# Four-layer convolution and scan network: order of work in layer 1's stream, one stream for layer 3, and the order of two ScalarE instructions

## The chip, the cores and the metric

The kernel runs on one core of a Trainium2 chip. The metric is the device time of one execution in microseconds (us), and the time that counts is the median of several executions. Five engines take part, each with its own instruction queue in program order: TensorE (PE in the profile, its weight loads PEld), VectorE (DVE), ScalarE (ACT), GpSimd (POOL) and SyncE (SP), which here does nothing but issue DMAs. An instruction waits on semaphores until what it needs is there, and everything behind it on its engine waits too. All data are float32.

## The reference, cut to what matters

The input is x of 8 x 64 x 64 x 64 (batch, channels, height, width). Four layers follow each other. Layer 0 (layer norm, FFTs, mixing) and the convolutional parts of layer 2 are not touched by the change. What the change touches are the selective scans. Layer 1 has this core, for 4 scan directions k of 8 images, 128 channels, 4096 tokens and 16 states:

```
xm = silu(dwconv3x3(ln(x) @ in_w)) ; z = second half of ln(x) @ in_w
dts, B, C = split(x_proj[k] @ xs[k]) ; delta = softplus(dt_w[k] @ dts + dt_b[k])
for each token: h = exp(delta*A)*h + delta*B*u ;  y = sum over states of h*C
y = ln(sum over the 4 directions of y + D*u) * silu(z) ; x1 = x + y @ out_w
x1 + conv1x1(gelu(h1) * h2)         # h1, h2 = dwconv3x3(conv1x1(ln(x1)))
```

Layer 3 has two stages, first along one axis of the image (s = 0), then along the other (s = 1). Stage 1 reads what stage 0 wrote. Each stage runs two Mamba blocks over sequences of 64 tokens, k = 0 forward and k = 1 backward, with 256 inner channels and 16 states:

```
xn = rms_norm(x) ; xc, z = split(xn @ in_w[k]) ; xc = silu(causal_conv(xc))
dts, B, C = split(xc @ xproj[k]) ; dt = softplus(dts @ dtw[k] + dtb[k])
h = h*exp(dt*A) + dt*xc*B ; y = (sum over states of h*C + D*xc) * silu(z)
out = concat(x + y0 @ out_w0, x + y1 @ out_w1) @ lin + linb + x
```

## The kernel before, in words

The whole network is one Python program that writes out every engine's instructions by hand. The scans of layers 1, 2 and 3 share the function `stream` (from L428 on). Its unit is a **tile**: one of the 16 states (n = 0 to 15) of one **step**, 128 channels x 1024 tokens (in layer 3 two halves of 512 tokens, one per half of the 256 channels). For tile i the stream issues:

- SP loads B's and C's row of this state, broadcast to 128 partitions. In layer 1 these are two loads of 512 KB, `b` by `fetch` (5 tiles ahead, 4 buffers) and `c` by `fetch_c` (3 tiles ahead, 5 buffers); in layers 2 and 3 one load brings both, and `fetch_c` does nothing.
- GpSimd multiplies `hb = du * b` (L484), 2 tiles ahead in layer 1 and 3 in the others.
- ScalarE computes `dA = exp(dt * A[n])` into PSUM (L491), 2 tiles ahead, in two buffers.
- VectorE scans `h = dA * h + hb` (L500).
- `h * C` (L514, `multiply_c`) is done by VectorE, except in the tiles called shared (n = 1, 4, 7, 10, 13 as a rule; 2, 6, 10, 14 in one step out of four in layer 3), where GpSimd does it one tile later.
- TensorE adds the product into the step's sum `acc` by a matmul with the identity (L306, `gather`), two tiles later. After the 16th tile VectorE takes the sum out (`drain`).

The next step's inputs are made while the present one is scanned: `prepare` is a Python generator that is advanced one piece per tile from n = `start` on (2 in layer 1, 1 in layer 3). It issues projection matmuls, ScalarE's copy `dbl`, the store of B and C to DRAM, softplus (`dt`), GpSimd's `du = dt * u` and, in layer 3, the matmuls of z and Silu(z).

Everything else in a layer is cut into pieces as well and queued as tasks in `behind`: in layer 1 `begin` (norm, convolution and z of an image ahead), `finish` (output norm, gate and projection of a finished image) and `feed` (its feed-forward part); in layer 3 `begin` (squares, mean, reciprocal root and `xn` of the next chunk; a chunk is 4 groups x 2 directions = 8 steps = 128 tiles). `advance` moves the first task on by one piece, once per tile. A piece ends in a `yield`, whose value says whether the task holds the shared PSUM buffer `mm` (True), needs one next (None), or neither (False). A task that said True is kept in `self.held`; no other work takes that buffer before it is done. `room` says whether a piece may take or hold PSUM in this tile: not while the preparation holds it. At n = `start` the preparation needs the buffer, so the loop `while self.held or self.urgent` runs the held task on, piece after piece in the same tile, until it lets go. These forced pieces stand ahead of the tile's scan in VectorE's queue. `late` is True for layer 1 alone, and there `early` is 8.

The pieces of layer 1 that the prediction names: L364 and L1065 are matmuls ahead of VectorE's L1011, L1104 and L1067; L1062 is a GpSimd product that L1067 also needs. In `feed`, a group is three matmul pieces (L917 twice, then L925), an empty piece, and its consumer: Gelu on ScalarE (L1130), a VectorE product (L1133), or Gelu (L1141), an empty piece and a VectorE product (L1144).

Layer 3 is the function `l3_stage`, called once per stage (L1815, L1816). Each call opens its own pools, loads and builds its weights, zeroes its buffers `raw` and `inv`, runs `begin(0)` to its end, and then runs a stream of 256 steps. At the end of `prepare` (L2013 to L2017) ScalarE first overwrites the last token of each sequence in `dt` with 1e30 (so that exp gives 0 there and the scan starts afresh at the next sequence), and then computes Silu(z). The overwriting must wait until `du` has been computed from the true `dt`.

The functions that the diff touches, with the profile's line numbers:

Of the kernel before, what the change touches and what calls it, by code (L numbers as in the profile page):

```python
# [268 lines left out]
class Net:  # L269
# [163 lines left out]
    def stream(self, pools, ahead, steps, behind, rest=None):  # L433
# [105 lines left out]
        for i in range(total + 2):  # L539
            at, n = divmod(i, NS)  # L540
            need(i + ahead[0], "bc")
            need(i + ahead[1], "du")
            fetch(i + ahead[0])
            fetch_c(i + ahead[2])
            multiply_b(i + ahead[1])
            if 0 < i <= total and shared(i - 1):
                multiply_c(i - 1)


            first = i > NS and n == 2  # L550
            late = i > 1 and not first and steps[0].late and shared(i - 2)
            if i > 1 and not late and not first:
                gather(i - 2)
            if at + 1 < len(steps) and n == steps[at].start:
                steps[at + 1].ready()
                while self.held or self.urgent:
                    self.advance(behind)
                work = Task(steps[at + 1].prepare())
            if work is not None and not (self.held and work.said is None) and (calm(i) or not work.calm):
                work.step()  # L560
                if work.over:
                    work = None
            room = work is None or work.said is not True and (n < steps[0].early or hasattr(steps[at + 1], "du"))
            self.advance(behind, room, calm(i))
            if late:
                gather(i - 2)
            if i < total:
                scan(i)
            if first:
                gather(i - 2)  # L570
            if i < total:
                if not shared(i):
                    multiply_c(i)
            decay(i + 2)
# [1239 lines left out]
    def layer3(self, src, dst):  # L1814
        self.l3_stage(0, src, self.hbm["x4"])  # L1815
        self.l3_stage(1, self.hbm["x4"], dst)  # L1816

    def l3_stage(self, s, src, dst):
# [5 lines left out]
        W, H = 512, 512 // HW  # L1824
        with ExitStack() as ctx:
            pool = lambda n, b, **k: ctx.enter_context(tc.tile_pool(name=f"l3{s}{n}", bufs=b, **k))
# [5 lines left out]
            def stage(name):  # L1832

                w = self.d["l3_" + name][:, 2 * s : 2 * s + 2]
                t = cp.tile(list(w.shape), F32, name="w_" + name)
                nc.sync.dma_start(t, w)
                return t

            linb = self.load(cp, "l3_linb")
            nw, w_in, cb, xp, dtw, dtb, A, D, w_out = (  # L1840
                stage(n) for n in ("nw", "in", "cb", "xp", "dtw", "dtb", "A", "D", "out")
            )
            lin = stage_lin = cp.tile([C, 2, C], F32, name="w_lin")
            nc.sync.dma_start(stage_lin, self.d["l3_lin"][:, s])
            self.minus_exp(A)
            nc.vector.tensor_scalar(A, A, -1e-27, None, ALU.min)
            skip = [self.diag(cp, f"skip{k}", D[:, k, :], 2) for k in range(2)]


            taps = [cp.tile([128, 2, 256], F32, name=f"taps{k}") for k in range(2)]  # L1850
            w_z = cp.tile([C, 2, 256], F32, name="w_z")
            w_end = cp.tile([128, 2, 2, C], F32, name="w_end")
            for k in range(2):
                for m in range(2):
                    for r in range(2):
                        row = self.d["l3_taps"][2 * s + k, m, r : r + 1, :]
                        nc.sync.dma_start(taps[k][r * C : r * C + C, m, :], row.to_broadcast([C, 256]))
                for m in range(2):
                    nc.vector.scalar_tensor_tensor(
                        taps[k][:, m, :], w_in[:, k, :256], nw[:, k : k + 1], taps[k][:, m, :], ALU.mult, ALU.mult  # L1860
                    )
                nc.vector.tensor_scalar(w_z[:, k, :], w_in[:C, k, 256:], nw[:C, k : k + 1], None, ALU.mult)

                for j in range(2):
                    ps = pp.tile([128, T], F32, name="mm")
                    nc.tensor.matmul(ps[:, :C], w_out[:, k, j * 128 : j * 128 + 128], lin[:, k, :], start=True, stop=True)
                    nc.scalar.copy(w_end[:, k, j, :], ps[:, :C])
            w_res = cp.tile([C, C], F32, name="w_res")
            nc.vector.tensor_tensor(w_res, lin[:, 0, :], lin[:, 1, :], ALU.add)
            nc.vector.tensor_tensor(w_res, w_res, self.ident[:C, :C], ALU.add)  # L1870
# [3 lines left out]
            nc.vector.memset(endless, 1e30)  # L1874

# [8 lines left out]
            def begin(c):  # L1884
# [4 lines left out]
                hold = chunks[c] = {"x": x}  # L1889
                from_ = src[q, rows, part * 4 * W : (part + 1) * 4 * W].rearrange("p (s t) -> p s t", t=HW)  # L1890
# [5 lines left out]
                for j in range(2):  # L1896
                    yield CALM_FREE
                    sq = p1.tile([C, T], F32, name="sq")
                    o = sq.rearrange("p (s t) -> p s t", t=HW)
                    nc.scalar.activation(o, x[:C, j * 2 * H : (j + 1) * 2 * H, ends[0]], AF.Square)  # L1900
                    yield
                    ps = pp.tile([128, T], F32, name="mm")
                    self.mm(ps[:1, :], mean, sq)
                    yield CALM
                    ms = p1.tile([1, T], F32, name="ms")
                    nc.scalar.copy(ms, ps[:1, :])
                    yield False
                    nc.sync.dma_start(rs[j * 64 : j * 64 + 64], ms.rearrange("o (p e) -> o p e", e=16))
# [30 lines left out]
            class Step:  # L1939
# [6 lines left out]
                def __init__(self, c, g, k):  # L1946
                    self.c, self.g, self.k, self.rev = c, g, k, k == 1
                    self.shared = (2, 6, 10, 14) if k and g % 2 else (1, 4, 7, 10, 13)
                    self.lanes = [(slice(j * W, j * W + W), A[:, k, j, :]) for j in range(2)]

                def ready(self):

                    while begun.get(self.c) in behind:
                        net.advance(behind)

                def prepare(self):
                    k, hold = self.k, chunks[self.c]
# [6 lines left out]
                    for j in range(2):  # L1964
                        for m, f in enumerate((4, 6) if k else (3, 1)):
                            nc.tensor.matmul(  # L1966
                                tokens(px[:, j * W : j * W + W]),
                                taps[k][:, m, j * 128 : j * 128 + 128],
# [7 lines left out]
                    for j in range(2):  # L1976
                        at = slice(j * W, j * W + W)
                        nc.scalar.activation(u[:, at], px[:, at], AF.Silu, bias=cb[:, k, j : j + 1])  # L1978
                    pd = pp.tile([128, T], F32, name="mm")[:36, :W]
                    for j in range(2):  # L1980
                        nc.tensor.matmul(pd, xp[:, k, j, :], u[:, j * W : j * W + W], start=j == 0, stop=j == 1)  # L1981
# [7 lines left out]
                    for j in range(2):  # L1989
                        nc.tensor.matmul(  # L1990
                            pt[:, j * W : j * W + W], dtw[:, k, j * 128 : j * 128 + 128], dbl[0:4], start=True, stop=True
# [4 lines left out]
                    for j in range(2):  # L1996
                        at = slice(j * W, j * W + W)
                        net.softplus_act(dt[:, at], pt[:, at], dtb[:, k, j : j + 1])
# [4 lines left out]
                    for j in range(2):  # L2003
                        nc.tensor.matmul(
                            tokens(pz[:, j * W : j * W + W]),
                            w_z[:, k, j * 128 : j * 128 + 128],
                            xn[:C, :, 3 : 3 + HW],
# [4 lines left out]
                    yield CALM  # L2012

                    at = HW - 1 if k else 0
                    nc.scalar.copy(dt.rearrange("p (s t) -> p s t", t=HW)[:, :, at], endless)
                    z = self.z = p2.tile([128, T], F32, name=f"z{k}")
                    nc.scalar.activation(z, pz, AF.Silu)  # L2017
# [5 lines left out]
                def skip(self, acc):  # L2023
                    for j in range(2):
                        at = slice(j * W, j * W + W)
                        nc.tensor.matmul(acc[:, at], skip[self.k][:, j, :], self.u[:, at], start=True, stop=False)
                    return True

                def drain(self, acc):
                    nc.vector.tensor_tensor(self.z, acc, self.z, ALU.mult)  # L2030
                    chunks[self.c][f"y{self.k}"] = self.z

                def done(self):
                    c, g = self.c, self.g
                    if self.k == 1:
                        net.urgent.append(Task(finish(c, g, [chunks[c]["y0"], chunks[c]["y1"]])))
                    if self.k == 0 and g == 0 and c + 1 < 2 * NB:
                        begun[c + 1] = Task(begin(c + 1))
                        behind.append(begun[c + 1])

            def finish(c, g, ys):
# [3 lines left out]
                x = chunks[c]["x"][:C, g * H : g * H + H, ends[0]]  # L2045
                nc.tensor.matmul(ps.rearrange("p (s t) -> p s t", t=HW), w_res, x, start=True, stop=False)  # L2046
                for k in range(2):
                    for j in range(2):
                        nc.tensor.matmul(  # L2049
                            ps, w_end[:, k, j, :], ys[k][:, j * W : j * W + W], start=False, stop=k == 1 and j == 1  # L2050
# [5 lines left out]
                if first:  # L2056
                    images[b] = p1.tile([C, L if s == 0 else 4 * W], F32, name="out")
# [10 lines left out]
            net = self  # L2068
            with tc.manual_schedule():
                Task(begin(0)).run()  # L2070
                steps = [Step(c, g, k) for c in range(2 * NB) for g in range(4) for k in range(2)]
# [27 lines left out]
```

## Time and profile before

| | us |
|---|---|
| median of 3 runs | 24834.52 (24824.01 to 24847.65) |
| the profiled execution's own time | 24819.55 |
| its span, first to last instruction | 24817.8 |
| layer 0 and the start of layer 1 | 0 to 1230 |
| layer 1, scan tiles (2,048) | 1230 to 8477 |
| rest of layer 1 and layer 2's first part | 8477 to 8957 |
| layer 2, scan tiles (512) | 8957 to 10617 |
| layer 2's last parts, start of layer 3 | 10617 to 11521 |
| layer 3, stage 0, scan tiles (2,048) | 11521 to 18125 |
| between the stages | 18125 to 18202 |
| layer 3, stage 1, scan tiles (2,048), and the end | 18202 to 24818 |

Busy time of the engines in three of these stretches, with the granted TensorE clock (1 is full speed) and the rate of the DMAs:

| stretch | length | PE | DVE | ACT | POOL | clock | GB/s |
|---|---|---|---|---|---|---|---|
| layer 1, tiles | 7247 | 6152 | 6656 | 3910 | 6728 | 0.93 | 317 |
| layer 3, stage 0 | 6604 | 5711 | 6409 | 4477 | 6511 | 0.95 | 170 |
| between the stages | 77 | 35 | 6 | 19 | 18 | 0.61 | 94 |

How such lines are read. A line of a view in order of time has the start and the length in us, the engine, the line of the kernel, the operation, what it writes and what it reads, a count (several of a kind are merged), and in brackets how long the engine stood idle before it and what released it. A line of the waits has who waited, for whom, the total in us, how often, and the longest. The page has, per engine, busy us, share of the span and number of instructions, and a digit string with the busy share in tenths in 40 slices of 620 us.

### The profile page before, as it was taken

How to read it: one execution, taken by the hardware profiler on the slowest of the kernel's cores; microseconds unless marked ns; L12 is line 12 of the kernel's file. 1: busy time of each engine (PE TensorE's matmuls, PEld its weight loads, DVE VectorE, ACT ScalarE, POOL GpSimd, SP SyncE). 2: the span in 40 equal slices, each digit the busy share in tenths (PEclk: the TensorE clock that was granted, in tenths of full speed). 3: DMA queues.
4: the chain of work that ended last, by engine and by line, in shares of the span. 5: the costliest groups of instructions: out<-in, count | busy, mean ns of one | idle time of the engine just before them, and what ended most of it. 6: DMA issues, size and time to landing. Idle time of an engine off the chain costs nothing. (4 is left out here: it accounts for less than half of the span.)

```text
span 24817.8 us, 193238 instructions
## 1 busy us (share of the span) xinstructions
PE 21209.1 (85%) x53146; PEld 8277.5 (33%) x53146; DVE 22437.6 (90%) x12958; ACT 14770.8 (60%) x18827; POOL 22097.5 (89%) x10583
## 2 busy tenths in 40 slices
PE   8877888888888888888888888888878888888888
PEld 6522333333333323322333333333323333333333
DVE  5399999999999679978999999999989999999999
ACT  4355555555555456624666666666666666666666
POOL 0199999999999669977999999999989999999999
PEclk9889999999999999999999999999989999999999
DMA  2399899899889669933455555555545554555454
GB/s 65 88 324 326 310 320 319 310 319 318 313 315 317 225 224 344 339 87 98 168 172 169 173 169 171 169 173 170 168 156 173 168 173 167 173 168 174 168 173 158
DMA packets 1835374, 5282.70 MB, mean 213 GB/s; under 512 B 533792, under 2 KB 540004, under 8 KB 1831984
## 3 DMA queue, kind: packets, MB, share of 16 engines
q1 hardware_dynamic: 1809712, 5207.00, 61.9%
q10 hardware_dynamic: 24576, 63.33, 0.7%
q8 instruction: 423, 6.93, 0.1%
q14 instruction: 663, 5.43, 0.1%
HBM read 5112.85 MB, written 156.11 MB: 212 GB/s over the span
## 5 line engine op out<-in xcount | busy, mean ns | idle before, releaser
L484 POOL TENSOR_TENSOR hb<-du,bc 128x1024 f32<-128x1024 f32 x4608 | 10745.6, 2359 | 201.3 <-DVE h L500 142.5
L306 PE MATMUL acc<-hc,ident 128*128 128x512 f32 x18560 | 8793.2, 615 | 109.8 <-DVE img L1266 61.4
L491 ACT ACTIVATE dA<-dt,w_A 128x512 f32<-128x512 f32 x8192 | 5655.4, 691 | 3950.7 <-DVE hc L514 2884.6
L500 DVE TENSOR_TENSOR_SCAN dA<-dA,hb 128x1024 f32<-128x1024 f32 x3320 | 7578.5, 2283 | 227.9 <-ACT dA L491 151.0
L306 PE MATMUL acc<-h,ident 128*128 128x512 f32 x8064 | 4623.7, 702 | 2390.1 <-POOL h L514 2361.7
L306 PEld LDWEIGHTS acc<-hc,ident 128*128 128x128 f32 x18560 | 3641.3, 200 | 5245.3 <-issue 4558.1
L484 POOL TENSOR_TENSOR hb<-du,b 128x1024 f32<-128x1024 f32 x2048 | 4837.5, 2395 | 460.4 <-DVE dA L500 220.7
L514 DVE TENSOR_TENSOR hc<-dA,bc 128x1024 f32<-128x1024 f32 x3232 | 3956.3, 1224 | 245.6 <-issue 5.8
L491 ACT ACTIVATE dA<-dt,w_l_A 128x1024 f32<-128x1024 f32 x2560 | 2857.1, 1117 | 1002.4 <-DVE hc L514 762.6
L500 DVE TENSOR_TENSOR_SCAN h<-dA,hb 128x1024 f32<-128x1024 f32 x1416 | 3229.2, 2280 | 148.2 <-ACT dA L491 144.8
L306 PEld LDWEIGHTS acc<-h,ident 128*128 128x128 f32 x8064 | 1560.4, 211 | 5100.2 <-POOL h L514 3403.4
L514 POOL TENSOR_TENSOR h<-h,bc 128x1024 f32<-128x1024 f32 x1376 | 3242.3, 2356 | 14.2 <-DVE h L500 14.2
L500 DVE TENSOR_TENSOR_SCAN dA<-dA,carry,hb 128x1024 f32<-128x1024 f32 x1320 | 3093.1, 2343 | 83.2 <-ACT dA L491 31.1
L514 DVE TENSOR_TENSOR hc<-dA,c 128x1024 f32<-128x1024 f32 x1408 | 1723.5, 1224 | 141.9 <-DMA c<-bc 32.0
L514 POOL TENSOR_TENSOR h<-h,c 128x1024 f32<-128x1024 f32 x640 | 1521.6, 2378 | 9.5 <-ACT carry L1249 8.9
L491 ACT ACT_TABLE_LOAD x1126 | 1444.7, 1283 | 20.0
L500 DVE TENSOR_TENSOR_SCAN h<-dA,carry,hb 128x1024 f32<-128x1024 f32 x600 | 1404.5, 2341 | 31.8 <-ACT dA L491 22.0
L1249 ACT COPY carry<-dA 128x1 f32<-128x1 f32 x1056 | 167.6, 159 | 1675.2 <-DVE hc L514 1635.5
L1966 PE MATMUL mm<-xn,taps 128*128 128x512 f32 x2048 | 939.1, 600 | 34.3 <-POOL xn L1930 31.1
L721 POOL MEMSET xf<- 128x24 f32 x33 | 4.3, 142 | 857.0 <-PE ps L742 728.0
L2001 POOL TENSOR_TENSOR du<-dt,u 128x1024 f32<-128x1024 f32 x256 | 602.8, 2355 | 18.5 <-ACT dt L415 18.5
L1981 PE MATMUL mm<-u,w_xp 128*36 128x512 f32 x1024 | 489.8, 601 | 149.2 <-ACT u L1978 140.1
(320 smaller groups left out, 18515.0 us busy)
## 6 DMA issues: line engine op xcount, KB each, us to landing
bc<-bc SPq DMA_DIRECT2D x4096, 512.0 KB
b<-bc SPq DMA_DIRECT2D x2048, 512.0 KB
c<-bc SPq DMA_DIRECT2D x2048, 512.0 KB
bc<-bc SPq DMA_DIRECT2D x512, 1024.0 KB
tmp<-rs SPq DMA_DIRECT2D x93, 512.0 KB
raw<-x SPq DMA_DIRECT2D x64, 512.0 KB
inv<-rs SPq DMA_DIRECT2D x64, 512.0 KB
tmp<-x SPq DMA_DIRECT2D x192, 128.0 KB
```

The costliest lines, as they stand in the source:

```text
L306: self.nc.tensor.matmul(o, lhsT, r, start=start, stop=stop)
L484: nc.gpsimd.tensor_tensor(s.shaped(hb[i]), s.shaped(s.du), B.pop(i), ALU.mult)
L491: nc.scalar.activation(dA[i][:, cut], s.dt[:, cut], AF.Exp, scale=A[:, n : n + 1])
L500: nc.vector.tensor_tensor_scan(h[:, way], dA[i][:, way], hb.pop(i)[:, way], s.first(n), ALU.mult, ALU.add)
L514: engine.tensor_tensor(s.shaped(o), s.shaped(h), CC.pop(i), ALU.mult)
L721: nc.gpsimd.memset(x[:, :, HW:], 0.0)
L1249: nc.scalar.copy(self.carry[:, n : n + 1], h[:, last : last + 1])
L1966: nc.tensor.matmul(tokens(px[:, j * W : j * W + W]), taps[k][:, m, j * 128 : j * 128 + 128], xn[:, :, f : f + HW], start=m == 0, stop=m == 1,)
L1981: nc.tensor.matmul(pd, xp[:, k, j, :], u[:, j * W : j * W + W], start=j == 0, stop=j == 1)
L2001: nc.gpsimd.tensor_tensor(du, dt, u, ALU.mult)
```

## The change

In `stream`, `fetch_c` is called ahead of `fetch`, which has an effect only in layer 1. In layer 1, two tiles (`left` = 2 and 1, that is n = 0 and n = 1) ahead of a preparation a held task is advanced by two pieces per tile instead of one, and in the tile just ahead of it no task that needs PSUM may begin.

In layer 3 the two stages become one stream of 512 steps. The weights of both stages are objects of a class `Weights`, loaded and built before the stream; large temporary ones use buffers of the `bc` pool. The first chunk's x is fetched ahead of stage 0's weights. The next chunk's `begin` is now also queued across the seam (`more`), so that stage 1's chunk 0 is prepared during stage 0's last chunk. To fit both sets of weights, `sq` and `ms` of `begin` share one buffer, z's weights share one with `dtw` and lie on partitions 64 to 127, so that z's matmuls read the upper half of `xn` (the same tokens, one column further), and the four small matmuls of the output weights share one PSUM tile and one copy. In `prepare`, Silu(z) is issued ahead of the overwriting of the sequences' ends.

```diff
@@ stream
             need(i + ahead[1], "du")
+            fetch_c(i + ahead[2])
             fetch(i + ahead[0])
-            fetch_c(i + ahead[2])
             multiply_b(i + ahead[1])
...
             room = work is None or work.said is not True and (n < steps[0].early or hasattr(steps[at + 1], "du"))
+
+            left = steps[at].start - n if at + 1 < len(steps) else 0
+            if left == 1 and steps[at].late and not self.urgent:
+                room = room and self.held is not None
             self.advance(behind, room, calm(i))
+            if 1 <= left <= 2 and steps[at].late and self.held:
+                self.advance(behind, room, calm(i))
             if late:
                 gather(i - 2)
@@ layer3
-        self.l3_stage(0, src, self.hbm["x4"])
-        self.l3_stage(1, self.hbm["x4"], dst)
-
-    def l3_stage(self, s, src, dst):
...
+        srcs, dsts = (src, self.hbm["x4"]), (self.hbm["x4"], dst)
...
+            class Weights:
...
+                def load(self):
+                    s = self.s
+
+                    spare = pools[0].tile([128, 2, W], F32, name="bc")
+                    self.w_in = pools[0].tile([128, 2, W], F32, name="bc")
+                    self.w_out = self.take("out", spare[:C, 0, :].rearrange("p (k t) -> p k t", k=2))
+                    self.lin = spare[:C, 1, : 2 * C].rearrange("p (k t) -> p k t", k=2)
+                    nc.sync.dma_start(self.lin, net.d["l3_lin"][:, s])
+                    self.nw = self.take("nw")
+                    self.take("in", self.w_in)
...
+                    self.cb, self.xp = self.take("cb"), self.take("xp")
+
+                    both = cp.tile([128, 2, 256], F32, name=f"both{s}")
+                    self.dtw, self.z = self.take("dtw", both[:4]), both[C:]
+                    self.dtb, self.A, self.D = self.take("dtb"), self.take("A"), self.take("D")
+
+                def build(self):
...
+                    self.end = cp.tile([128, 2, 2, C], F32, name=f"w_end{s}")
+                    nc.scalar.copy(self.end.rearrange("p k j o -> p (k j o)"), ps)
...
+                    net.minus_exp(self.A)
...
@@ begin
-                    sq = p1.tile([C, T], F32, name="sq")
+
+                    both = p1.tile([128, T], F32, name="sq")
+                    sq, ms = both[:C], both[C : C + 1]
...
-                    ms = p1.tile([1, T], F32, name="ms")
@@ prepare
                         nc.tensor.matmul(
                             tokens(pz[:, j * W : j * W + W]),
-                            w_z[:, k, j * 128 : j * 128 + 128],
-                            xn[:C, :, 3 : 3 + HW],
+                            w.z[:, k, j * 128 : j * 128 + 128],
+                            xn[C:, :, 4 : 4 + HW],
...
                     yield CALM
+                    z = self.z = p2.tile([128, T], F32, name=f"z{k}")
+                    nc.scalar.activation(z, pz, AF.Silu)
+
 
                     at = HW - 1 if k else 0
                     nc.scalar.copy(dt.rearrange("p (s t) -> p s t", t=HW)[:, :, at], endless)
-                    z = self.z = p2.tile([128, T], F32, name=f"z{k}")
-                    nc.scalar.activation(z, pz, AF.Silu)
@@ done
-                    if self.k == 0 and g == 0 and c + 1 < 2 * NB:
-                        begun[c + 1] = Task(begin(c + 1))
-                        behind.append(begun[c + 1])
+                    more = self.s * 2 * NB + self.c + 1
+                    if self.k == 0 and self.g == 0 and more < 4 * NB:
+                        at = divmod(more, 2 * NB)
+                        begun[at] = Task(begin(*at))
+                        behind.append(begun[at])
@@ layer3, the end
-                Task(begin(0)).run()
-                steps = [Step(c, g, k) for c in range(2 * NB) for g in range(4) for k in range(2)]
+                first = Task(begin(0, 0))
+                first.step()
+                weights[0].load()
+                weights[0].build()
+                first.run()
+                weights[1].load()
+                weights[1].build()
+                steps = [
+                    Step(s, c, g, k) for s in range(2) for c in range(2 * NB) for g in range(4) for k in range(2)
+                ]
                 self.stream(pools, (6, 3, 6), steps, behind)
```

## The prediction

> **What bounds the kernel now.** The page comes first, for where time can be lost at all.
>
> ```profile
> PE 21209.1 (85%) x53146; PEld 8277.5 (33%) x53146; DVE 22437.6 (90%) x12958; ACT 14770.8 (60%) x18827; POOL 22097.5 (89%) x10583
> DVE  5399999999999679978999999999989999999999
> POOL 0199999999999669977999999999989999999999
> ```
>
> VectorE and GpSimd share the work of every scan tile and are busy 90% and 89%. A gain is idle time taken out of both. The page's chain of waits breaks off at 0% after the last few us and is no help. The slices show a dip in the 30th, inside layer 3. VectorE's instructions in order of time show it:
>
> ```profile
> 18122.39 2.27 DVE L500 TENSOR_TENSOR_SCAN dA<-dA,hb 128x1024 f32<-128x1024 f32 x1
> ...
> 18202.53 2.30 DVE L500 TENSOR_TENSOR_SCAN dA<-dA,hb 128x1024 f32<-128x1024 f32 x1 [33.67 <-ACT dA L491]
> ```
>
> These are the last scan of stage 0 and the first of stage 1: 80.1 us from start to start, where neighbours are 2.2 to 3.5 apart. Then VectorE's waits in layer 1 (1230 to 8477; columns: total us, times, longest):
>
> ```profile
> DVE tmp L1133 <- PE mm L925: 71.9, 28, 6.6
> DVE tmp L1144 <- ACT tmp L1141: 69.7, 13, 5.4
> DVE tmp L1067 <- POOL tmp L1062: 51.6, 22, 3.4
> DVE hc L514 <- DMA c<-bc: 32.0, 19, 4.0
> ```
>
> GpSimd waits there mostly for VectorE (`hb`, 220.7 and 188.9 us): the two block each other through three `hb` buffers, so a VectorE stall is nearly a stall of the layer. Last, layer 3's prefix of a step, ScalarE and then VectorE in order of time:
>
> ```profile
> 13879.94 0.22 ACT L2015 COPY dt<-endless 128x16 f32<-128x16 f32 x1 [2.33 <-POOL du L2001]
> 13880.18 1.28 ACT L2017 ACT_TABLE_LOAD   x1
> 13881.47 1.02 ACT L2017 ACTIVATE z<-mm 128x1024 f32<-128x1024 f32 x1
> ```
>
> ```profile
> 13885.32 2.29 DVE L500 TENSOR_TENSOR_SCAN h<-dA,hb 128x1024 f32<-128x1024 f32 x1 [2.14 <-ACT dA L491]
> ```
>
> ScalarE stands 2.33 us for GpSimd's `du`, and its late `dA` then stops VectorE for 2.14.
>
> **Part 1, one stream in layer 3: -72 us, and +5 at its start.** Scan starts 128 tiles apart (one chunk) are 413.0 us apart in both stages, 414.2 for the very first; a last chunk, in which no next chunk is prepared, takes 407.1 and 405.9. Layer 3 runs from its first scan at 11520.9 to the last one's end at 24803.1: 13282.2 us. As one stream it is 414.2 + 30 x 413.0 + 405.9 = 13210.1. The 72.1 between them is the hole less one usual distance (about 3) and the 6 us that preparing chunk (1,0) costs inside the stream, as for any other chunk. What stood in the hole goes (stage 1's weights, 5.84 us of GpSimd memsets, the drain and refill) or moves ahead of the stream. What moves is weights[1]: SP issues (14 us for such a set, 18135.1 to 18149.1), 4 matmuls, some 4 us of VectorE. At layer 3's start SP's `inv` loads end at 11491.8 and its next issue is at 11509.4, so the 14 us fit; VectorE is idle there for 32.8. Not hidden is ScalarE: the Exp of A now stands in front of `u`. A's load is next to last of the set, so it lands about 11508, then table load 1.28, Exp and scale 0.52, Silu's table 1.28 (today loaded early, at 11487.9): `u` starts near 11510.6 instead of 11505.55, **+5** (0 to +10). x being fetched ahead of the weights saves 2; sq of the second half waiting for ms's DMA costs 2. If the seam's cover were gone (stage 1 waiting for x4 to be complete), 72 come back.
>
> Of the sharing of one buffer by sq and ms: in the stream sq starts 1.22 us after the DMA's issue, which lands 1.4 to 2.5 after it by the packets; ScalarE's next `dA` is idle 2.27 us there, so 31 times up to 1.3 us lie hidden: **0** (at most +20). z's matmuls on the upper half of `xn` (same elements one column on, 64 rows either way): **0**.
>
> **Part 2, the ends behind z's Silu: -59 us.** The copy needs `du`, Silu needs only its matmuls, done at 13877.94 while ScalarE is free at 13877.62. So table load 1.28 + Silu 1.02 = 2.3 us run inside the wait of 2.33. By tile, the stage's VectorE waits of this kind are 27.3 us in 15 sixth steps and 24.0 in 15 seventh steps of a chunk, 3.4 per chunk: where GpSimd falls back because of `xn`. What is late next is GpSimd: its `hb` is ready only 1.9 us before its scan at the tightest tiles of those two steps. So VectorE can come 1.9 forward, no more. That is paid out in the eighth step, where GpSimd today waits for VectorE 29.4 us in 15 chunks, 1.96 each. 31 x 1.9 = **-59** (0 if absorbed; -105 if all 3.4 counted).
>
> **Part 3, c ahead of b on SP, layer 1: -20 us.** c(i+3) needs multiply_c(i-2). On VectorE tiles that is long done, and c leaves one GpSimd operation (2.36) earlier: the 32.0 us of waits for c go. On the five shared tiles of 16 it is a GpSimd operation behind the one that b waits for, and behind c on SP now stand b and all of the layer's other loads: 2.36 later. GpSimd waits for b. Taking each landing from the DMA's closing packets, 638 moved b loads land 6.8 us (median) ahead of use; 13 of them land less than 2.36 ahead, and the shortfall sums to 12. -32 + 12 = **-20** (-32 to +23, the shortfall at 3 us with nothing gained).
>
> **Part 4, double pace, layer 1: -18 us.** I stepped the loop's order through all 2,048 tiles. Before, 65 tiles with n = 2 force work out in front of the preparation: 13 times Gelu L1141 with its consumer L1144 right behind it (the trace has exactly 13 waits, 5.3 each), 7 times six matmuls L925 with L1133 (38.9), 7 L1067 (16.0), 7 L1011 (4.5): 129 us in all. After, 7 are left, each one L1144. But the work lands elsewhere, with one tile between matmul and consumer where it had two. For each place I took from the trace when the producer ends against when VectorE is free there:
> - L1144: 7 behind n = 2, Gelu one tile ahead, 5 each (3.7 to 6.4): 35; 21 elsewhere, 0.
> - L1133: 14 at n = 9, where six matmuls issued at n = 7 end 2.4 late (up to 4.8): 34; 7 at n = 14, 1.9 each: 13; 7 at n = 0: 0.
> - L1067: 7 at n = 1, L1062 ends 4.4 late: 31; the rest as now, 40.
> - L1011 and L1104, 6 each at n = 1, matmuls end 2.75 late: 33.
>
> Together 186, against 203.6 for these lines now (71.9 + 69.7, L1067's 51.6 + 4.7, L1011's 4.5, L1104's 1.2): **-18** (-150 if the new places cost nothing, +50 at their upper ends). ScalarE's late `dA` is about even: fewer pieces at n = 2 and n = 9, more at n = 1.
>
> **A rule against it.** A table load's row is 1283 ns, and 13623.17 + 1.28 is followed by Silu at 13624.47: 20 ns later. The Trainium skill, ScalarE: Activation LUTs, What ACT_TABLE_LOAD costs, adds a drain and puts every switch to another set at about 2.66 us. The double pace puts 14 Gelu or Silu pieces at n = 1, two switches each: 28 x 1.38 = +39, which would turn part 4 from -18 to +21, and part 1's start from +5 to +8. No such gap stands in this trace; I use the row.
>
> **Sum.** -72 + 5 - 59 - 20 - 18 = -164. The profiled execution took 24819.55 (span 24817.8), so 24656; the median shown is 15 above it, hence **24671**.
>
> **Rivals.**
> - B, the double pace pays in full (14%): the waits at n = 2 vanish and the new places have slack. For: steps with a forced L1133 or L1144 last 60 to 61 us against 55 to 57 of their neighbours. Against: matmuls are late at n = 7 to 9 already. -129 for -18: 24560.
> - C, only the seam counts (17%): part 2 ends in a wait for `hb`, layer 1 stays even. For: 1.9 us of slack is thin, parts 3 and 4 each have ends of both signs. -67: 24767.
> - D, the stream does not close the seam (5%): chunk (1,0)'s reading of x4 or the image buffer holds it up. Against: x4's first image was written 6 ms before. 24671 + 72 = 24743.
> - E, slower (6%), by one mechanism: SP stands at c in layer 1 and b comes too late for GpSimd. It outweighs the rest and 0.2% only when the moved loads cost some 195 us; by the landings that needs a shift of about 5.2 us, not 2.36. Priced at 6 us, over 250 us lost: above 24884.
>
> **How the numbers follow.** My forecast has 58%, its own range 24620 to 24725. A measurement here tells apart about 0.2%, 50 us. The range 24560 to 24785 holds all of mine, C nearly whole, D and half of B; left out are E, half of B and a bit of C, under 2 in 10. Faster by over 0.2% (below 24785): mine, B, D, and 11 of C's 17, with one taken off, 87%. Same: the rest of C, 7%. Slower: 6%.
>
> **What would show it.** Part 1: consecutive scans with no hole, layer 3 near 13150 us with part 2 included. Part 2: L2015's wait (118.5 us) near 0, GpSimd's waits for VectorE in the eighth step gone. Part 3: no wait for c, waits for b up by some 10 us. Part 4: forced L1144 down from 13 to 7, new waits of L1133 (n = 9) and L1067 (n = 1). I am wrong if layer 1 moves by more than 80 us, or if `hb` becomes what VectorE waits for in layer 3.

## The result and the profile after

The changed kernel takes 24812.13 us (median of 20 runs, 24789.79 to 24820.34); the kernel before took 24841.74 in the same series. The ratio is 0.9987 with an interval of 0.9981 to 0.9993: some 30 us less, inside the 0.2% that the forecast called "same". The forecast was 24671, with a range of 24560 to 24785. The profiled execution took 24810.32 (span 24808.5), 9 less than the one of before, which lay 22 below its median.

The pieces of the two spans, from first scan to last scan's end of each layer:

| piece | before | after | difference | forecast |
|---|---|---|---|---|
| start to layer 1's first scan | 1229.8 | 1230.7 | +1 | 0 |
| layer 1, scan tiles | 7246.6 | 7301.1 | **+54** | **-38** (parts 3 and 4) |
| to the end of layer 2's scans | 2140.8 | 2143.7 | +3 | 0 |
| to layer 3's first scan | 903.7 | 905.6 | +2 | +5 |
| layer 3, scan tiles | 13282.2 | 13212.7 | **-69** | **-131** (-72 part 1, -59 part 2) |
| tail | 14.6 | 14.7 | 0 | 0 |

So two things failed, one in each layer. First VectorE's row of the page, which has VectorE busy 91% and GpSimd 89% of the span:

```profile
DVE  5399989999999769978999999999999999999999
```

The dip in the 30th slice is gone. VectorE in order of time, where stage 0 ends and stage 1 begins:

```profile
18189.11 2.27 DVE L500 TENSOR_TENSOR_SCAN dA<-dA,hb 128x1024 f32<-128x1024 f32 x1
...
18192.62 2.29 DVE L500 TENSOR_TENSOR_SCAN dA<-dA,hb 128x1024 f32<-128x1024 f32 x1
```

The first line is the last scan of stage 0, the last one the first scan of stage 1: 3.5 us apart, where it was 80.1. But the usual chunk, 128 tiles, is still 413.0 us in both stages. VectorE's waits in layer 3's stage 0 (total us, times, longest), before and then after:

```profile
DVE h L500 <- ACT dA L491: 60.9, 46, 2.2
...
DVE z L2030 <- PE acc L306: 19.8, 30, 2.4
```

```profile
DVE z L2075 <- PE acc L306: 53.5, 43, 3.9
DVE h L500 <- ACT dA L491: 27.1, 32, 2.2
```

The wait for ScalarE's `dA` fell by 33.8 us, and the wait of the drain (L2030, now L2075) for the finished sum rose by 33.7. (In stage 1 the first fell from 59.2 to 30.7 and the second rose from 18.2 to 41.8.) By place, in stage 0: the 27.3 and 24.0 us at n = 13 of the sixth and seventh steps are gone; new are 13.1 and 28.1 (5.2 before) at the drains at n = 2 of the seventh and eighth, and 14.8 for a late `dA` at n = 10 of the seventh.

VectorE's waits in layer 1 after the change (lines are six further down: L1139 was L1133, L1150 was L1144, L1073 was L1067, L1110 was L1104, L1017 was L1011):

```profile
DVE dA L500 <- ACT dA L491: 142.4, 92, 4.4
DVE tmp L1139 <- PE mm L931: 93.7, 28, 5.7
...
DVE tmp L1073 <- POOL tmp L1068: 51.8, 25, 4.3
...
DVE tmp L1150 <- ACT tmp L1147: 25.1, 7, 3.6
DVE tmp L1110 <- PE mm L364: 24.2, 9, 5.5
...
DVE tmp L1017 <- PE mm L364: 19.7, 7, 3.9
...
DVE tmp L1073 <- PE mm L306: 14.7, 4, 4.7
...
DVE hc L514 <- DMA c<-bc: 5.3, 1, 5.3
```

The wait for c went as forecast (32.0 to 5.3), and L1150 has its 7 waits. But the five lines of the double pace together went from 203.6 to 230 us, and the scans' waits (L500) for ScalarE's `dA` and `carry` from 175 to 213, of which `dA` is 16 of the added 38 and `carry`, the last column of a tile that ScalarE keeps for the next step, 22. GpSimd pays for the new order of the loads in layer 1; its waits for b were 19.3:

```profile
POOL hb L484 <- DMA b<-bc: 70.0, 55, 5.7
```

### The profile page after: what moved, and what is told of

Its sections match the earlier page's. It is cut to its first block, busy times and chain, and to the rows that moved or that the text cites. A ratio compares the mean times of both kernels' runs of the same rounds, so it can differ in the third digit from the quotient of the medians.

```text
span 24808.5 us, 192860 instructions
## 1 busy us (share of the span) xinstructions
PE 21260.8 (86%) x53146; PEld 8293.9 (33%) x53146; DVE 22456.3 (91%) x12956; ACT 14801.9 (60%) x18824; POOL 22128.2 (89%) x10580
## 5 line engine op out<-in xcount | busy, mean ns | idle before, releaser
L500 DVE TENSOR_TENSOR_SCAN dA<-dA,hb 128x1024 f32<-128x1024 f32 x3320 | 7581.0, 2283 | 214.2 <-ACT dA L491 103.7
L484 POOL TENSOR_TENSOR hb<-du,b 128x1024 f32<-128x1024 f32 x2048 | 4914.7, 2462 | 481.9 <-DVE h L500 183.6
L500 DVE TENSOR_TENSOR_SCAN h<-dA,hb 128x1024 f32<-128x1024 f32 x1416 | 3229.1, 2280 | 91.3 <-ACT dA L491 80.4
L500 DVE TENSOR_TENSOR_SCAN dA<-dA,carry,hb 128x1024 f32<-128x1024 f32 x1320 | 3093.6, 2344 | 135.9 <-ACT dA L491 68.8
L514 POOL TENSOR_TENSOR h<-h,c 128x1024 f32<-128x1024 f32 x640 | 1557.9, 2434 | 29.1 <-ACT carry L1255 28.5
L500 DVE TENSOR_TENSOR_SCAN h<-dA,carry,hb 128x1024 f32<-128x1024 f32 x600 | 1404.6, 2341 | 13.3 <-ACT carry L1255 13.3
```

Source lines behind the costliest of these rows:

```text
L484: nc.gpsimd.tensor_tensor(s.shaped(hb[i]), s.shaped(s.du), B.pop(i), ALU.mult)
L500: nc.vector.tensor_tensor_scan(h[:, way], dA[i][:, way], hb.pop(i)[:, way], s.first(n), ALU.mult, ALU.add)
L514: engine.tensor_tensor(s.shaped(o), s.shaped(h), CC.pop(i), ALU.mult)
```

## The experiments

All kernels are the changed one with the edit shown, unless said otherwise. In the traces, layer 1's scan tiles take 7247 and 7250 us in the two kernels that have the order of before, and 7293 to 7310 in the six that have the order of the change, so under some 15 us nothing is read from one trace. Layer 3 is steadier: five kernels with the change's layer 3 and an altered layer 1 take 13212.3 to 13218.2.

### Layer 1: which part costs

**Both parts undone** (b first again; both `left` rules out):

```diff
-            fetch_c(i + ahead[2])
             fetch(i + ahead[0])
+            fetch_c(i + ahead[2])
...
-            if left == 1 and steps[at].late and not self.urgent:
-                room = room and self.held is not None
...
-            if 1 <= left <= 2 and steps[at].late and self.held:
-                self.advance(behind, room, calm(i))
```

> Layer 3 as in the change, layer 1's stream as before (b ahead of c, one held piece per tile, work may begin at n = 1). If layer 1's part of the change is what cost the time, its scan tiles are back at 7247 us (7301 with the change), layer 3 stays at 13213, and the time is 24812 - 54 = about 24758, some 80 below the kernel before. If instead the longer layer 1 came from something else in the program (the chip's clock, the place of buffers), layer 1 stays near 7301 and the time near 24812.

Layer 1 takes 7249.7, layer 3 13212.3, the whole 24780.04 (ratio 0.9971, 0.9960 to 0.9981). The longer layer 1 is the work of parts 3 and 4 and of nothing else in the program. The median is 67 below the 24847.53 that the kernel before took in the same series.

**b ahead of c, double pace kept** (only the first hunk above):

> The change with b fetched ahead of c again; the double pace stays. Order theory (c ahead of b makes b late for GpSimd, whose waits for b rose from 19 to 70 us): layer 1 falls from 7301 to 7230 to 7250, the time to 24745 to 24760, and VectorE's 32 us of waits for c come back. Pace theory (the pieces that now stand at n = 0, 1, 8 and 15 make TensorE and ScalarE late): layer 1 stays at 7290 to 7320.

Layer 1 takes 7287.4, the time is 24815.12 (0.9988, 0.9981 to 0.9994). GpSimd's waits for b are back at 20.5, and layer 1 is still 38 longer than in the kernel with both parts undone (35 by the medians; the profiled execution was the fastest of 19). The order theory falls as the main cause.

**Single pace, c ahead of b** (the other two hunks alone):

> The change without the double pace and without the rule that no work begins at n = 1; c stays ahead of b. Order theory: layer 1 stays at 7285 to 7300, GpSimd's waits for b stay near 70 us. Pace theory: layer 1 falls to 7220 to 7250, VectorE's waits for c stay near 5 us. If each did half of the harm, both this kernel and the one with b ahead lie near 7275.

Layer 1 takes 7251.2, the time is 24778.72 (0.9972, 0.9962 to 0.9982). GpSimd's waits for b:

```profile
POOL hb L484 <- DMA b<-bc: 55.2, 60, 3.4
```

The forced places are as before the change (the old L1133 and L1144 have 71.2 and 69.7 us for 71.9 and 69.7), and GpSimd still waits 55 us for b. So the new order of c and b takes 27 us of waits for c from VectorE, gives it 29 us of waits for `hb` back, and makes no difference that can be read (+1.5 us). The double pace together with the rule for n = 1 is what costs: by the traces +50 with c first and +38 with b first, by the medians (each against the kernel before in its own series) +39 and +35.

**Double pace without the rule for n = 1**, and **the rule without the double pace** (one of the two hunks each):

> The change without the rule that no work begins at n = 1; two pieces per tile in the two tiles ahead of a preparation stay, c stays ahead of b. Stepping the loop gives 48 tiles with forced work: 13 times L1144 alone, 7 times Gelu with L1144, 6 times six matmuls with L1133. At what the runs show for such places (3.6, 5.3 and 6.5 us each) these are 123 us, and the one-tile distances at n = 0 and 1 of L1067, L1011, L1133 stay, some 70. Pace theory (the short distance from matmul to consumer costs, not the rule): layer 1 at 7300 to 7330. If the rule is what costs (work held back at n = 1 comes late elsewhere): 7240 to 7260.

> The change with the rule that no work begins at n = 1, but one piece per tile as before; c stays ahead of b. Stepping the loop gives 29 tiles with forced work, with every matmul two tiles ahead of its consumer but 7 of L1144 whose Gelu stands at n = 2 and 13 whose Gelu stands at n = 1 or before. Pace theory: layer 1 at 7225 to 7255, the waits of L1067, L1011 and L1104 as in the kernel before (61 us together), L1144 at 37 to 85. If the rule is what costs: 7285 to 7300.

Double pace alone: layer 1 7327.5, time 24829.03 (0.9996, 0.9988 to 1.0004). The rule alone: 7253.9, 24753.66 (0.9966, 0.9953 to 0.9978). With c ahead of b in all four, the table has the length of layer 1, VectorE's waits at the forced and near places (L1133, L1144, L1067, L1011, L1104 of before), the scans' waits for ScalarE's `dA` and `carry`, and the median of the time against the kernel before in the same series, in us:

| kernel | layer 1 | forced and near places | late `dA`, `carry` | median |
|---|---|---|---|---|
| single pace, work may begin at n = 1 | 7251.2 | 202 | 171 | -69 |
| double pace, work may begin at n = 1 | 7327.5 | 297 | 157 | -11 |
| single pace, not at n = 1 | 7253.9 | 164 | 211 | -86 |
| double pace, not at n = 1 | 7301.1 | 230 | 213 | -30 |

The second piece per tile costs 47 to 76 us by the traces and 57 to 58 by the medians, whatever stands beside it. It shows at the forced and near places, whose waits grow by 95 and 66. The double pace alone has the forced places that stepping the loop had given, 20 of them at Gelu's product, with 98.5 us. The rule takes 38 and 67 us from such places and gives 40 and 56 back as late `dA` and `carry`; by the medians it saves 17 and 19, which is within their noise. So the late `dA` and `carry` come with the rule and not with the double pace. VectorE's waits in the kernel before, and then with the rule alone:

```profile
DVE dA L500 <- ACT dA L491: 102.0, 82, 2.8
DVE h L500 <- ACT dA L491: 46.7, 29, 4.3
DVE dA L500 <- ACT carry L1249: 16.2, 25, 2.2
DVE h L500 <- ACT carry L1249: 9.8, 10, 2.0
```

```profile
DVE dA L500 <- ACT dA L491: 114.6, 91, 4.3
DVE h L500 <- ACT dA L491: 48.3, 26, 6.1
DVE dA L500 <- ACT carry L1253: 25.1, 25, 2.9
DVE h L500 <- ACT carry L1253: 22.9, 16, 2.0
```

Against the single pace without the rule, 38 of the 40 us stand at n = 11 to 13. Just ahead of them, with the rule, ScalarE has, over the whole layer, 14 instead of 6 copies into `strip` (L933) at n = 11 and 8 instead of 1 of its pieces L1036 at n = 10; that these are the reason was not tried. The clock is not what tells the four kernels apart: in layer 1 TensorE was granted 0.92 with the rule alone (7253.9) and 0.93 with the double pace alone (7327.5), and 0.93 and 0.92 in the kernels with neither and with both.

What such a place looks like, in the changed kernel: TensorE and VectorE in order of time, in the tiles n = 7 to 9 of one step:

```profile
3802.52 1.88 PE L306 MATMUL acc<-h,ident 128*128 128x512 f32 x4
3804.24 1.88 PE L306 MATMUL acc<-hc,ident 128*128 128x512 f32 x4
3806.05 2.85 PE L931 MATMUL mm<-strip,hright 64*128 64x512 f32 x12
```

```profile
3803.50 1.23 DVE L514 TENSOR_TENSOR hc<-dA,c 128x1024 f32<-128x1024 f32 x1
3808.94 1.22 DVE L1139 TENSOR_TENSOR tmp<-mm,tmp 128x1024 f32<-128x1024 f32 x1 [4.21 <-PE mm L931]
3810.08 2.35 DVE L500 TENSOR_TENSOR_SCAN dA<-dA,carry,hb 128x1024 f32<-128x1024 f32 x1
```

TensorE does not pause here: one row starts where the one before ends. It has eight matmuls of the scan's sums in its queue ahead of L931 (and the feed-forward's earlier ones ahead of these), and VectorE stands 4.21 us at L1139, with the tile's scan behind it, until TensorE is through. This group comes to n = 9 by the rule: with the rule alone these 14 places cost 55.8 us, in the changed kernel 51.8, with the double pace alone there is one, of 4.6. Clearing the tile of the preparation put this group where TensorE had a queue.

### Layer 3: where the gain of the Silu went

**The old order of copy and Silu:**

```diff
-                    z = self.z = p2.tile([128, T], F32, name=f"z{k}")
-                    nc.scalar.activation(z, pz, AF.Silu)
                     at = HW - 1 if k else 0
                     nc.scalar.copy(dt.rearrange("p (s t) -> p s t", t=HW)[:, :, at], endless)
+                    z = self.z = p2.tile([128, T], F32, name=f"z{k}")
+                    nc.scalar.activation(z, pz, AF.Silu)
```

> The change with the copy of the sequences' ends ahead of z's Silu again. GpSimd theory (what VectorE gained in the sixth and seventh steps it lost at the drains, which wait for GpSimd's h*C through TensorE): chunks stay at 413.0 us and layer 3 at 13213, with the old waits of 27 and 24 us back at n = 13 and the waits at the drains of the seventh and eighth steps gone; the time is the change's. Offset theory (the new order is worth the forecast 59 us and something else in layer 3 cost as much): chunks of 414.9, layer 3 at about 13270.

The usual chunk is 413.0 again, layer 3 takes 13215.3, the time is 24815.00 (0.9989, 0.9982 to 0.9995). The waits at n = 13 are back with 30.9 and 25.7 us, and the drain's have shrunk:

```profile
DVE h L500 <- ACT dA L491: 68.7, 47, 2.2
DVE z L2075 <- PE acc L306: 19.6, 29, 5.6
```

Part 2 is worth nothing that can be read, and the offset theory falls. What the drain waits for, in the changed kernel: GpSimd, TensorE and VectorE at the end of one seventh step:

```profile
14008.27 2.33 POOL L514 TENSOR_TENSOR h<-h,bc 128x1024 f32<-128x1024 f32 x1
```

```profile
14010.66 2.08 PE L306 MATMUL acc<-h,ident 128*128 128x512 f32 x2 [3.34 <-POOL h L514]
```

```profile
14018.92 1.23 DVE L2075 TENSOR_TENSOR z<-acc,z 128x1024 f32<-128x1024 f32 x1 [2.36 <-PE acc L306]
```

GpSimd does tile 13's h\*C without having waited for anything since the fourth step. TensorE adds the tiles in order, so it stands 3.34 us for this one, with the sums of tiles 14 and 15 behind it, and VectorE's drain waits for the last of them.

**One of GpSimd's products moved out of this stretch.** If GpSimd sets the pace from the fifth step to the eighth, work taken from it there must shorten the chunk, though VectorE gets it:

```diff
-                    self.shared = (2, 6, 10, 14) if k and g % 2 else (1, 4, 7, 10, 13)
+                    self.shared = (2, 6, 10, 14) if k and g >= 2 else (1, 4, 7, 10, 13)
```

> The change, with one of GpSimd's h*C products in layer 3 moved from the sixth step of a chunk to the fourth (the steps with four shared tiles are now the sixth and the eighth, no longer the fourth and the eighth; as many shared tiles in all). GpSimd theory (from the middle of the fifth step to the drain of the seventh GpSimd never waits, and its h*C products hold TensorE's sums and so VectorE's drain, 41 us of waits per stage): GpSimd reaches the drain one product of 2.34 us earlier, VectorE's waits for acc at the drains of steps 6 and 7 fall from 41 us to under 15, a chunk goes from 413.0 to 411 to 412 us, the time 30 to 70 below the change's. Rival (VectorE's waits there come from ScalarE's late dA, and GpSimd's lateness is beside the point): chunks stay at 413.0, or grow by up to 1.2 where VectorE gets the product back.

The usual chunk is 409.6 us, layer 3 takes 13125.1, the time is 24726.13 (0.9952, 0.9938 to 0.9965). VectorE's waits at the drains in stage 0 fall from 53.5 us to 14.3; at those of steps 6 and 7 there are 2.2 left of 41. GpSimd's own waits in stage 0, in the changed kernel and then here:

```profile
POOL hb L484 <- DVE h L500: 65.3, 53, 2.1
POOL hb L484 <- DVE dA L500: 20.9, 28, 1.6
```

```profile
POOL hb L484 <- DVE h L500: 35.8, 34, 2.1
POOL hb L484 <- DVE dA L500: 5.3, 3, 3.3
```

They fall from 86 us to 41, 2.8 per chunk, which is most of the 3.4 by which the chunk is shorter. The 34 us in the fourth step, where GpSimd used to wait and now has the product, are all gone. The chunk was expected to gain 1 to 2 us and gained 3.4. The edit also moves the other products of both steps (2, 6, 10, 14 for 1, 4, 7, 10, 13), and with them the pieces of ScalarE that stay out of tiles next to a shared one; what the places alone are worth was not tried for this edit.

This holds beyond the one edit. GpSimd has the same products to make in a chunk of every kernel here. Take from each usual chunk the time that GpSimd waits in it: 407.5 to 407.8 us are left (medians) in the kernel before, in the changed one and in all the others, with chunks from 409.6 to 418.2. A change in this loop is worth what it takes from GpSimd's waits, 5.2 us per chunk before the change. The new order of copy and Silu left them at 5.3.

**The same with the copy first again:**

> The change with one shared product moved from the sixth to the fourth step of a chunk, and the copy ahead of z's Silu again. If GpSimd alone hid the worth of the new order, it shows now that GpSimd is out of the way: chunks 1.5 to 3.5 us longer than the 409.6 of the kernel that only moves the product, layer 3 at 13170 to 13235. If the order of the two ScalarE instructions is worth nothing in itself, 409.6 and 13125 stay.

Chunks of 409.6, layer 3 at 13117.9, the time 24720.33 (0.9954, 0.9941 to 0.9968). The order is worth nothing here either. But this does not show that it has no worth in itself, because GpSimd is not out of the way: it now waits almost only at n = 7 of a chunk's eighth step and n = 5 of its first, some 2 us per chunk, and what VectorE does earlier between these two does not shorten GpSimd's row.

**GpSimd's products earlier in these steps**, as many as before, with Silu first and with the copy first:

```diff
                     self.shared = (2, 6, 10, 14) if k and g % 2 else (1, 4, 7, 10, 13)
+                    if (g, k) in ((2, 1), (3, 0)):
+                        self.shared = (1, 3, 4, 7, 10)
```

> The change, with GpSimd's five h*C products of the sixth and the seventh step of a chunk in layer 3 at n = 1, 3, 4, 7, 10 in place of 1, 4, 7, 10, 13: as much work for GpSimd, but none of it right ahead of the drain. Drain theory (VectorE's lead of 1.9 us from the new order is lost only because the sum of the step waits for the product of n = 13): waits for acc at the drains of these steps fall from 41 us per stage to under 10 and a chunk goes from 413.0 to 411.0 to 412.2. Pace theory for GpSimd (it is busy without a pause there, so VectorE meets it at one place or another): the waits move to hb, and chunks stay at 412.6 or above.

> The same early products, with the copy of the ends ahead of z's Silu again. Drain theory: VectorE's late dA at n = 13 is now what counts, so chunks are 1 to 2 us longer than with Silu first. Pace theory for GpSimd: the same length within 0.3 us, whichever of the two ScalarE instructions is first.

The times are 24970.83 (1.0050, 1.0033 to 1.0067) and 24977.49 (1.0055, 1.0040 to 1.0070), and the usual chunks of stage 1 take 416.2 to 416.7 us in both (in stage 0 they take 416 to 423). The waits at the drains of the sixth and seventh steps are gone, as the drain theory wanted; the chunk is longer all the same. With Silu first, 58.4 us in stage 0 and 51.7 in stage 1 are now waits for `dA` at n = 8 of the seventh step. TensorE, ScalarE and VectorE there:

```profile
20297.94 2.79 PE L306 MATMUL acc<-h,ident 128*128 128x512 f32 x4 [3.21 <-POOL h L514]
20300.65 2.76 PE L2027 MATMUL mm<-u,w_xp 128*36 128x512 f32 x4
```

```profile
20303.45 0.58 ACT L2030 COPY dbl<-mm 36x512 f32<-36x512 f32 x1 [4.09 <-PE mm L2027]
20303.93 2.74 ACT L491 ACTIVATE dA<-dt,w_A 128x512 f32<-128x512 f32 x4
```

```profile
20305.42 2.30 DVE L500 TENSOR_TENSOR_SCAN dA<-dA,hb 128x1024 f32<-128x1024 f32 x1 [3.69 <-ACT dA L491]
```

The product that TensorE awaits has changed its place, so the wait has changed its name: GpSimd holds TensorE, TensorE holds ScalarE's copy `dbl`, and the `dA` behind that copy holds VectorE. So the drain alone was not the obstacle, and the waits went to `dA`, not to `hb` as the pace theory had it. What both theories differ on most, the order of copy and Silu, makes no difference that can be read here either (0.2 us per chunk), for the third time. The run does not price the drain by itself, since the edit also shifts other pieces of ScalarE.

### All that helped, together

The moved product in layer 3, single pace without the rule in layer 1, and this order of the loads:

```diff
+            early_c = i < 2 or not shared(i - 2)
+            if early_c:
+                fetch_c(i + ahead[2])
             fetch(i + ahead[0])
+            if not early_c:
+                fetch_c(i + ahead[2])
```

> Three things at once, in stretches that do not touch: layer 3 with one shared product moved from the sixth to the fourth step; layer 1 at single pace without the rule; c ahead of b only in tiles where the product that frees c's buffer is VectorE's (on the five where it is GpSimd's, b goes first). Layer 3 should take 13120 us. If b was late only because SP stood at a c that GpSimd had yet to free, GpSimd's waits for b fall from 55 us (single pace, c always first) to about 20 with VectorE's waits for c still near 5, and layer 1 goes from 7251 to 7225 to 7240: time about 24675. If b comes late because of the order of the transfers themselves, layer 1 stays near 7250 and the time near 24690.

24662.41 us (24650.40 to 24681.79), ratio 0.9929, interval 0.9916 to 0.9943: below both kernels. Layer 1 takes 7232.5, layer 3 13132.4. GpSimd's waits for b:

```profile
POOL hb L484 <- DMA b<-bc: 24.0, 24, 2.7
```

So b was late mostly because SP stood at a c whose buffer GpSimd had yet to free. VectorE's waits for c are 18.4, not the 5 expected, and the 19 us by which layer 1 is shorter than with c always first are little above what one trace can tell.

## Why the prediction was wrong, step by step

The forecast was -164 between the two profiled executions, measured were -9. Of the 155 us between them, layer 1 (parts 3 and 4) has 92 and part 2 some 60.

- **Part 1, the seam: right.** Forecast -72 and +5. Layer 3 is 69.5 shorter with chunks of unchanged length, its first scan comes 1.9 later, and the first chunk takes 417.0 for 414.2 (415.1 to 415.3 in four of the five kernels with the same layer 3). Together -68 for -67. The ScalarE delay at the start was somewhat too large an estimate (its terms add up to 11511.1, not 11510.6, so to 5.5); sharing `sq` and `ms`, and z on the upper half, cost nothing that shows.
- **Part 2, -59: wrong, 0.** The local step was right: the waits at n = 13 went. The step that failed is "its `hb` is ready only 1.9 us before its scan ... so VectorE can come 1.9 forward". It took `hb` for the only thing through which GpSimd holds VectorE. GpSimd also makes h\*C of five tiles in sixteen, and these pass through TensorE to the drain and to ScalarE's next `dA`. Of VectorE's 33.8 us in stage 0 and 28.5 in stage 1, 33.7 and 23.6 came back at the drain. The profile of before had the warning: the drain at n = 2 of the eighth step already waited in 9 of 16 chunks of stage 0, 5.2 us in all, so in these chunks its slack was not 1.9 but none. The second half of the step, that GpSimd's idle time in the eighth step would pay it out, failed with it: the 29.4 us (which were those of all 16 chunks, not of 15) became 32.9. Where the gain went is shown by the waits; what the order would be worth with GpSimd out of the way stays open, because in the sixth and seventh steps GpSimd does not wait at all in the kernel before, and under 4 us per stage in every kernel here.
- **Part 3, -20: off, nothing that can be read by itself (+1.5), nor beside the double pace and the rule (+14 by one pair of traces, +3 by the medians).** The 32 us of waits for c went (5.1 left). The term mis-sized is the shortfall of b, set at 12 for a shift of one GpSimd operation: GpSimd's waits for b rose by 36, and VectorE's for `hb` by 29. The cause named was right: letting b go first where c's buffer is GpSimd's to free brought GpSimd's waits for b down to 24. +23, the upper bound given, holds it.
- **Part 4, -18: wrong, +35 to +50.** The counts were right: 7 forced L1144, at 25 us for the 35 forecast. Of the new places L1067 took 66.5 (forecast 71) and L1011 and L1104 together 45 (forecast 33). The step that failed is L1133: 34 at n = 9, 13 at n = 14 and "7 at n = 0: 0" were 51.8, 12.9 and 29.0. Those at n = 9 come with the rule (55.8 with it alone), those at n = 0 with the double pace (28.4 with it alone). TensorE's queue at the new places had been taken from a trace in which those matmuls were not there, which is the likely reason but was not tried by itself. The other is "ScalarE's late `dA` is about even": +16 us for `dA` and +22 for `carry`, which no term had. The four kernels of the table put both on the rule that no work begins at n = 1; the prediction had taken rule and double pace as one. The upper end of +50 that it gave is what came.
- **The table loads.** The prediction's rule against it (the Trainium skill, ScalarE: Activation LUTs, What ACT_TABLE_LOAD costs) set +39 on this part, close to the +38 of late `dA` and `carry`. The agreement is by chance: after the change the load at 13940.35 starts 0.01 us after the instruction before it ends, takes 1.28, and the Silu starts at 13941.65, 0.02 later. Of this trace's 2337 table loads 2175 have less than 0.05 us of idle time on each side, so the drain that the page adds is not there, and the measurement decides. The 38 us came with the rule for n = 1 at single pace as well (40).
- **The rivals.** C, "only the seam counts", named part 2's end rightly in kind (a wait takes its place) and wrongly in name (`hb`). With layer 1 even it gave -67; the kernel with layer 1 as before took 67 less than the kernel before in its series. What no rival had is a layer 1 that loses 50. "I am wrong if layer 1 moves by more than 80 us, or if `hb` becomes what VectorE waits for in layer 3" missed on both counts: 54 in the wrong direction was enough, and the name was the drain's.

## What to carry to other kernels

When two engines share the work of a loop, slack has to be measured on every path by which one holds the other, those through a third engine and its in-order queue included; a wait at the end of such a path that is already there in some rounds is a warning that a gain ahead of it may be worth nothing. The engine to relieve is the one that never waits in the stretch: moving one of its products to where it did wait was worth 87 us here, where taking 62 us of the other engine's waits away was worth none. Work moved from one tile to another must be priced against the queue that it will find there, which the trace of before does not show. Where the bounds then lie 200 us apart, try it alone, and each of its rules alone, before it goes in with other parts.

## What was not expected of the hardware

GpSimd's products seem slower after the change: 2462 ns for 2395 in layer 1's row of `hb`.

```profile
L484 POOL TENSOR_TENSOR hb<-du,b 128x1024 f32<-128x1024 f32 x2048 | 4914.7, 2462 | 481.9 <-DVE h L500 183.6
```

(In the kernel before the row has 4837.5 us and 2395 ns.) From start to start, where the next one does not wait, they are 2335 ns apart for 2329. The recorded spans overlap by a median of 119 ns for 63, so most of the 67 ns by which a span is longer is not time lost. Over the kernels this distance has two values, 2329 to 2336 ns (the kernel before, the changed one, and it with b first, with single pace, with both undone, or with the copy first and nothing else) and 2352 to 2354 (all the others, the fastest among them). It follows no edit made here; its cause is open. It does not make the table of layer 1: between single and double pace the distance rises without the rule (2330 to 2352) and falls with it (2353 to 2335), and the double pace costs 57 to 58 us by the medians both times.
